# The first 256 tokens in two parts of 128: loads, norm and four small products

## The chip, the cores and the metric

The kernel runs on one core of a Trainium2 chip. The metric is the device time of one execution in microseconds (us). Engines: PE (TensorE, matrix products; PEld are its weight loads), DVE (VectorE), ACT (ScalarE), POOL (GpSimd) and SP (SyncE, which here only issues DMAs). SP and ACT each have a DMA queue of their own.

## The reference

`x` is 4 x 1024 tokens of 1024 features, float32. What matters of it:

```
xn = (x - mean) / sqrt(var + 1e-5)              # per token
g  = sigmoid(xn @ gate_w.T + gate_b)            # gate; then a linear recurrence over time gives s
h  = silu(silu(xn @ w1.T) @ w3.T) @ w2.T        # a small MLP, all 4096 tokens
p  = top-2 of softmax(xn @ wr.T), normed        # eight experts
out[expert] += p * h                            # adds to ROWS 0..7 of the output, by the expert's number
result = x + s * silu(out)                      # so only rows 0..7 differ from x
```

So nearly all work is in three products: `u` = xn by w1 and `m` by w3 over all tokens, and `g` by gate_w over the first 1024 tokens.

## The kernel before

**Tiles.** The tokens are taken in four groups of 1024. In each, a 1024 x 1024 x 1024 product is done as seven half-size products of sums and differences of quarters (i = 1 to 7, in the order 1, 2, 5, 6, 7, 4, 3), and most of these once more in seven. i = 1 of `u` is "plain": its eight small products are done as they are. A **small product** (`small`, L895) takes 256 tokens, 256 features and 256 output columns: four calls of `pe.matmul`, each with a stationary 128 x 128 of the weights and 256 moving token columns. Each call is two records in the profile, so a small product is 8 records. A `Half` (L911) holds one half-size product with its PSUM tiles `X`, `Z` and `Y`; its `step(n)` emits one small product and the DVE or ACT operation that takes the sum out of PSUM.

**The transposed input.** `xT` is stored with features along partitions. The block `first` (L1226), `[128, 4, 512]`, holds the first 512 tokens of the first 512 features: index 0 and 1 are token group 1 (tokens 0 to 255), 2 and 3 token group 2 (256 to 511). Each index has two tiles of 128 features ("k tiles") of 256 tokens. The features' mean and scale are per token, thus along the free axis here. To get them there, the statistics are taken from rows of `x` (tokens along partitions), a diagonal matrix is made of each (identity times the per-partition value), and a product of an all-ones matrix with the diagonal spreads the value over all partitions as a row in PSUM ("spread"). Then DVE subtracts the mean row and multiplies by the scale row (`on` in `first_tokens`, L359; `norm0`, L304).

**Order.** Every engine keeps the program's order (`Pinned`, L79). The order is written by hand: each step of a `Half` has a place (a number; `steps`, L1442), and `at(place, f)` puts anything else in a list that is emptied up to a place before the step of that place is emitted (`run_todo`, L191). A generator's `yield d` puts off its rest by `d` places. One place is about one small product.

**The start.** SP and ACT load `x_first` (rows 0 to 255 of `x`) in four pieces of 256 KB, two on each queue (L150). PE runs `warm(14)`, idle products on the identity (28 records), so that it is busy meanwhile (L1225). SP then loads, in this order (L1233 to L1240): index 0 of `first` (256 KB), half of the w1 block (the two indices 0 and 2, 512 KB), index 1 of `first`, the same half of the gate block, rows 256 to 511 of `x` in two pieces, the other halves of w1 and gate, indices 2 and 3 of `first`. From the ninth transfer on, SP waits before an issue until the transfer eight places before has landed (a wait on the same semaphore in the trace).

`first_tokens` (L317, place -10) then takes the statistics of all 256 tokens on DVE (four `bn_stats`, two `bn_aggr`), spreads mean and scale with `warm` products between, and norms index 0 and 1 in five DVE operations of 256 or 512 columns. `stats0` (L247) does the same for token group 2 at place -8, with its diagonals on ACT, and emits its two spreads 11.9 and 12.9 places later, so at places 3.9 and 4.9; `norm0` at 3.95 and 4.95 applies them, one DVE operation of 1024 columns each.

PE's small products in order: at places 0 and 1 `X_u` (two, accumulated), at 2 `X_g` and at 3 `Y_g`, all with token group 1 and the first halves of the weights; at 4 and 5 the two `Z_u`, with the second half of w1; at 6 and 7 the `X_u` of token group 2. ACT copies `X_u` and `X_g` out of PSUM after places 1 and 2; DVE adds `Y_g` at place 5.2. POOL's sums for later products (`first_sums`, `left_sums`) need the normed token group 2.

Of the kernel before, what the change touches and what calls it, by code (L numbers as in the profile page):

```python
# [10 lines left out]
F32 = mybir.dt.float32  # L11
# [5 lines left out]
P = 128  # L17
# [5 lines left out]
def kernel(  # L23
# [99 lines left out]
                self.home.append(self.tile)  # L123

    NB, NQ = 20, 18
    IDLE = 14
    blocks = deque(
        const.tile([P, 4, 2 * Q], F32, tag=f"b{i}", name=f"b{i}") for i in range(NB)
    )
# [18 lines left out]
    pool.memset(three_halves, 1.5)  # L148

    x_first = block()  # L150
    for n in range(2):
        for t, queue in ((0, sync), (1, act)):
            queue.dma_start(
                x_first[:, 2 * t + n, :], x[t * P : (t + 1) * P, n * H : (n + 1) * H]
            )

    root = const.tile([P, 1], F32, tag="root", name="root")
    act.activation(root, eps, AF.Sqrt)
# [83 lines left out]
    def part(t, a):  # L242
        return t[:, 2 * a : 2 * a + 2, :].rearrange("p b (k n) -> p (b k) n", n=Q)
# [3 lines left out]
    def stats0(I, a, xb, lag, wait=(0, 0), apart=0):  # L247

        mv = sp.tile([P, 2, 2], F32, tag="mv", name=f"mv_{I}{a}")
        for tt in range(2):  # L250
            xt = xb[:, 2 * tt : 2 * tt + 2, :]
            bn = sp.tile([P, 2, nc.vector.BN_STATS_DIM], F32, tag=f"bn{tt}", name=f"bn_{I}{a}{tt}")
            for n in range(2):
                dve.bn_stats(bn[:, n, :], xt[:, n, :])
            dve.bn_aggr(mv[:, tt, :], bn)
        xb.drop()
        dg = quarter()

        def diagonals(s, w):
            for tt in range(2):  # L260
                act.activation(
                    dg[:, (2 * s + tt) * P : (2 * s + tt + 1) * P],
                    ident,
                    AF.Identity,
                    scale=w[:, tt : tt + 1],
                )

        if (I, a) == (1, 1):
            bc = ps_sm.tile([P, 2, Q], F32, tag="sm", name="bc_11")
        elif (I, a) == (1, 0):  # L270
            bc = ps_y.tile([P, 2, Q], F32, tag="Y", name="bc_10")
        else:
            bc = acc.rearrange("p (s n) -> p s n", s=2)
        yield wait[0]

        sd, v, r1 = (bc[:, 1, 2 * i : 2 * i + 2] for i in range(3))
        act.activation(sd, mv[:, :, 1], AF.Sqrt, bias=eps)
        act.activation(v, mv[:, :, 1], AF.Identity, bias=eps)
        diagonals(0, mv[:, :, 0])
        r0 = sp.tile([P, 2], F32, tag="r2", name="r0")  # L280
        rs = sp.tile([P, 2], F32, tag="rs", name=f"rs_{I}{a}")
        dve.reciprocal(r0, sd)
        dve.reciprocal(r1, sd)
        dve.scalar_tensor_tensor(rs, r0, -0.5, r1, ALU.mult, ALU.mult)
        dve.tensor_mul(rs, rs, v)
        dve.scalar_tensor_tensor(rs, rs, 1.5, r1, ALU.add, ALU.mult)
        yield wait[1]
        diagonals(1, rs)
        yield lag
        for s in range(2):  # L290
            if s:
# [12 lines left out]
    def norm0(I, a, J, apart=0):  # L304
        p = part(xn[0, I, J], a)
        for s, op in ((0, ALU.subtract), (1, ALU.mult)):
            if s and apart:
                yield apart
            row = bc0[I, a][s].unsqueeze(1).to_broadcast([P, 4, Q])
            dve.tensor_tensor(p, p, row, op)  # L310

    def warm(n):

        for _ in range(n):
            pe.matmul(idle, ones, ident, start=True, stop=True, skip_group_check=True)

    def first_tokens():  # L317


        mv = sp.tile([P, 2, 2], F32, tag="mv", name="mv_00")  # L320
        bn = [
            sp.tile([P, 2, nc.vector.BN_STATS_DIM], F32, tag=f"bn{t}", name=f"bn_00{t}")
            for t in range(2)
        ]
        for n in range(2):
            for t in range(2):
                dve.bn_stats(bn[t][:, n, :], x_first[:, 2 * t + n, :])
        for t in range(2):
            dve.bn_aggr(mv[:, t, :], bn[t])
        x_first.drop()  # L330
        sd = sp.tile([P, 2], F32, tag="sd2", name="sd_00")
        act.activation(sd, mv[:, :, 1], AF.Sqrt, bias=eps)
        dg = quarter()
        rows = [
            ps_acc.tile([P, Q], F32, tag="rows", name="mean_00"),
            ps_sm.tile([P, Q], F32, tag="sm", name="scale_00"),
        ]
        bc0[0, 0] = rows

        def spread(s, w):  # L340
            d = dg[:, s * Q : (s + 1) * Q]
            for t in range(2):
                dve.tensor_scalar(
                    d[:, t * P : (t + 1) * P], ident, w[:, t : t + 1], None, ALU.mult
                )
            pe.matmul(rows[s], ones, d, start=True, stop=True, skip_group_check=True)

        spread(0, mv[:, :, 0])
        warm(2)
        v = sp.tile([P, 2], F32, tag="v2", name="v_00")  # L350
        dve.tensor_scalar(v, mv[:, :, 1], EPS, None, ALU.add)
        rs = sp.tile([P, 2], F32, tag="rs", name="rs_00")
        scales(rs, v, sd, 2)
        spread(1, rs)
        dg.drop()
        warm(3)
        p = part(xn[0, 0, 0], 0)

        def on(lo, hi, s, op):  # L359
            row = rows[s].unsqueeze(1).to_broadcast([P, hi - lo, Q])  # L360
            dve.tensor_tensor(p[:, lo:hi, :], p[:, lo:hi, :], row, op)

        on(0, 2, 0, ALU.subtract)
        on(0, 1, 1, ALU.mult)
        on(1, 2, 1, ALU.mult)
        on(2, 4, 0, ALU.subtract)
        on(2, 4, 1, ALU.mult)

    def stats(sb, bcs):

# [219 lines left out]
    def first_sums(t):  # L590

        for _ in fresh_sums("g", 1, t, False):
            yield 0.5
        yield 3
        for _ in left_sums("u", 0, 1, 1):
            yield 0.5

# [313 lines left out]
    class Half:  # L911
# [33 lines left out]
        def step(self, n):  # L945
# [9 lines left out]
            if self.plain:  # L955

                q = ((0, 1, 2, 3) if self.i == 1 else (0, 3, 1, 2))[n // 2]
                ps = self.X if n // 2 % 2 == 0 else self.Z
                go(ps, A[:, q // 2 * 2 + n % 2], t[:, n % 2 * 2 + q % 2], n % 2 == 0, n % 2 == 1)
                if n % 2:  # L960
                    self.first(q, ps)
            elif n == 0:
                go(self.X, A[:, 0], t[:, 0], True, False)
                self.first(0, self.X)
            elif n == 1:
                go(self.Z, s[0].tile, ts[0].tile, True, False)
                self.first(3, self.Z)
                s[0].drop()
                ts[0].drop()
            elif n == 2:  # L970
                go(self.X, s[1].tile, ts[1].tile, False, False)
                self.first(1, self.X)
                s[1].drop()
                ts[1].drop()
            elif n == 3:
                Y = ps_y.tile([P, 2 * Q], F32, tag="Y", name=f"Y_{self.tag}")
                go(Y, A[:, 1], t[:, 2], True, True)
                if (self.kind, self.i) == ("g", 1):
                    at(Y_AT, self.more, 0, Y)
                else:  # L980
                    self.more(0, Y)
            elif n == 4:
                go(self.X, s[2].tile, ts[2].tile, False, False)
                self.more(3, self.X)
                s[2].drop()
                ts[2].drop()
            elif n == 5:
                go(self.Z, s[3].tile, t[:, 3], False, True)
                self.more(1, self.Z)
                s[3].drop()  # L990
            elif n == 6:
                go(self.X, A[:, 3], ts[3].tile, False, True)
                self.first(2, self.X)
                self.whole(2)
                ts[3].drop()
# [237 lines left out]
    sync.dma_start(first[:, 0, :], xT[0, 0, 0, :, 0, :])  # L1233
    first_half("w1", 0)
    sync.dma_start(first[:, 1, :], xT[0, 0, 0, :, 1, :])
    first_half("gw", 0)
    load_x0(0, 1)
    first_half("w1", 1)
# [7 lines left out]
    at(-16, load_xn, 0, 1, 0, USES[1, 0] + G[1, 0])  # L1246
    at(-15, load_xn, 0, 1, 1, USES[1, 1] + G[1, 1])
    at(-10, first_tokens)
    at(-8, lambda: stats0(0, 1, x0[0, 1], 11.9, apart=1))
    at(3.95, norm0, 0, 1, 0, 1)  # L1250
    at(6, lambda: stats0(1, 0, x0[1, 0], 2.5, (1.5, 1)))
    at(6.5, norm0, 0, 0, 1)
    at(8.5, norm0, 0, 1, 1)
# [4 lines left out]
    at(18, norm0, 1, 1, 1)  # L1258
    at(26, consts)
    for IJ in HB:  # L1260
        at(0, lambda IJ=IJ: left.__setitem__(("u", 0, IJ), xn[(0,) + IJ]))

    halves = []
    for kind, sb, i, plain in line:
# [117 lines left out]
    def the_rest():  # L1382
# [60 lines left out]
        (at_first[kind, sb, i][n] if (kind, sb, i) in at_first else start[kind, sb, i] + 2 * n, k, n)  # L1443
        for k, (kind, sb, i, plain) in enumerate(line)
        for n in range(8 if plain else 7)
    )
    for place, k, n in steps:
        here[0] = place
# [81 lines left out]
```

## Time and profile before

| what | before |
|---|---|
| median of 3 runs | 820.97 us (820.76 to 821.0) |
| the profiled execution: its time | 820.79 us |
| its span on the core | 819.0 us |
| first real product on PE starts | 10.32 us |
| last record of PE starts | 814.43 us |
| DMA in the first 40 us | 381 GB/s |

The span is what the trace covers; some 1.8 us of the execution lie outside. All times below are from the span's start. In a timeline a line gives the start, the length, the engine, the source line, the operation with what it writes and reads, and how many records stand in the line; in brackets is the engine's idle time before it and what ended it. The recorded lengths of PE's products overlap: what counts there is the distance from one start to the next. All engine calls go through one helper, so that nearly every line has L89, and groups are told apart by the names of the tiles.

### The profile page before, as it was taken

The page shows a single profiled execution, that of the slowest core. Times are in us where ns is not written, and L with a number is a line of the kernel's source. Part 1 is how long each engine was busy: PE and PEld are TensorE (multiplying, and loading weights), DVE is VectorE, ACT ScalarE, POOL GpSimd, SP SyncE. Part 2 cuts the span into 40 slices and gives each one's busy share as a digit, 9 for nine tenths or more (in the row PEclk, how much of TensorE's full clock was granted, in tenths as well). Part 3 has the DMA queues.
Part 4 walks back from the last instruction along what each step waited for, and adds up shares of the span by engine and source line. Part 5 has one row for each costly group of instructions (what it writes and reads, how often), then busy time and mean ns, then how long its engine had stood idle before and what let it go on. Part 6 is the DMA issues. An engine that isn't in the chain of part 4 may idle for free.

```text
span 819.0 us, 11323 instructions
## 1 busy us (share of the span) xinstructions
PE 811.4 (99%) x4087; PEld 698.2 (85%) x4087; DVE 510.6 (62%) x872; ACT 267.3 (33%) x470; POOL 496.5 (61%) x398
## 2 busy tenths in 40 slices
PE   8999999999999999999999999999999999999997
PEld 7888888888888878888888788888888788888885
DVE  6986598765588534764985235666983246667643
ACT  2345126877233237341022065421122021220111
POOL 2799796957999394644547453754448454465300
PEclk9999999999999999999999999999999999999999
DMA  9946609464978958629955866559766355555700
GB/s 341 423 169 232 231 27 359 180 244 152 409 275 311 339 183 295 246 88 380 387 170 221 334 224 238 193 206 385 282 244 241 120 213 207 197 177 178 302 14 2
DMA packets 55927, 192.88 MB, mean 235 GB/s; under 512 B 6480, under 2 KB 9792, under 8 KB 44224
## 3 DMA queue, kind: packets, MB, share of 16 engines
q1 hardware_dynamic: 55552, 191.61, 63.6%
q8 instruction: 33, 0.54, 0.2%
q10 hardware_dynamic: 320, 0.54, 0.2%
q14 instruction: 22, 0.18, 0.1%
HBM read 169.01 MB, written 39.87 MB: 255 GB/s over the span
## 4 chain that ended last, share of the span: by engine, by line
PE 98%; DMA 1%; DVE 0%; issue 0%; SPq 0%; ACT 0%
PE X_u L89 24%; PE X_m L89 24%; PE Z_u L89 12%; PE Z_m L89 12%; PE Y_m L89 6%; PE X_g L89 6%; PE Y_u L89 6%; PE Z_g L89 3%; PE acc L89 2%; PE plT L89 2%; PE Y_g L89 1%; DMA b<-in_x 1%; PE pp L89 0%; PE bc L89 0%; DVE bn L89 0%; PE accB L89 0%
## 5 line engine op out<-in xcount | busy, mean ns | idle before, releaser
L89 POOL TENSOR_TENSOR q<-b 128x512 f32<-128x512 f32 x154 | 203.5, 1336 | 194.6 <-PE X_m L89 48.0
L89 ACT ACTIVATE b<-b 128x512 f32<-128x512 f32 (+1 forms) x152 | 105.4, 696 | 296.5 <-DVE b L89 292.5
L89 POOL TENSOR_TENSOR q<-b,q 128x512 f32<-128x512 f32 x98 | 133.7, 1368 | 7.2 <-issue 4.0
L89 POOL TENSOR_TENSOR b<-b,b 128x512 f32<-128x512 f32 x72 | 93.1, 1318 | 48.5 <-PE X_u L89 33.8
L89 DVE TENSOR_TENSOR b<-b,b 128x512 f32<-128x512 f32 x120 | 109.2, 924 | 2.7
L89 PE MATMUL X_m<-q,q 128*128 128x256 f32 x448 | 105.9, 379 | 0.0
L89 PE MATMUL X_u<-q,q 128*128 128x256 f32 x432 | 102.4, 380 | 0.0
L89 DVE TENSOR_TENSOR b<-X_u,b 128x512 f32<-128x512 f32 x87 | 60.1, 691 | 58.6 <-PE X_u L89 57.9
L89 DVE TENSOR_TENSOR b<-X_m,b 128x512 f32<-128x512 f32 x88 | 60.3, 687 | 56.9 <-PE X_m L89 56.6
L89 PEld LDWEIGHTS X_m<-q,q 128*128 128x128 f32 x448 | 85.0, 190 | 12.4 <-issue 0.8
L89 POOL TENSOR_TENSOR q<-q,b 128x512 f32<-128x512 f32 x56 | 73.7, 1317 | 32.3 <-PE X_u L89 25.1
L89 PEld LDWEIGHTS X_u<-q,q 128*128 128x128 f32 x432 | 81.8, 190 | 12.2 <-issue 1.2
L89 DVE TENSOR_TENSOR b<-b,bc 128x1024 f32<-128x1024 f32 x56 | 67.8, 1210 | 0.1
L89 PE MATMUL X_u<-b,b 128*128 128x256 f32 x248 | 58.4, 379 | 0.0
L89 PE MATMUL Y_m<-b,b 128*128 128x256 f32 x224 | 53.1, 380 | 0.0
L89 PE MATMUL Z_m<-b,q 128*128 128x256 f32 x224 | 53.0, 379 | 0.0
L89 PE MATMUL X_m<-b,b 128*128 128x256 f32 x224 | 52.9, 379 | 0.0
L89 PE MATMUL Z_m<-q,q 128*128 128x256 f32 x224 | 52.9, 379 | 0.0
L89 PE MATMUL X_m<-q,b 128*128 128x256 f32 x224 | 52.9, 379 | 0.0
L89 PEld LDWEIGHTS X_u<-b,b 128*128 128x128 f32 x248 | 47.0, 190 | 6.4
L89 DVE TENSOR_TENSOR b<-Z_u,b 128x512 f32<-128x512 f32 x47 | 32.5, 691 | 31.6 <-PE Z_u L89 30.9
L89 PE MATMUL Z_u<-q,q 128*128 128x256 f32 x216 | 51.1, 379 | 0.0
(182 smaller groups left out, 1179.2 us busy)
## 6 DMA issues: line engine op xcount, KB each, us to landing
q<-w SPq DMA_DIRECT2D x168, 256.0 KB, 4.5
b<-in_w SPq DMA_DIRECT2D x36, 1024.0 KB, 8.8
b<-w_T SPq DMA_DIRECT2D x24, 1024.0 KB, 6.2
b<-in_xT SPq DMA_DIRECT2D x15, 1024.0 KB, 11.6
w<-q SPq DMA_DIRECT2D x56, 256.0 KB, 7.1
b<-in_x SPq DMA_DIRECT2D x12, 1024.0 KB, 10.9
w_T<-b SPq DMA_DIRECT2D x8, 1024.0 KB, 4.4
b<-in_gw SPq DMA_DIRECT2D x6, 1024.0 KB, 15.6
```

Of the source, the lines that this page charges most:

```text
L89: r = f(*args, **kwargs)
```

## The change

`x_first` is loaded in another order: rows 0 to 127 come first, one piece on SP and one on ACT; the two pieces of rows 128 to 255 come later on SP, behind the first half of w1 and index 1 of `first`, and ahead of the gate half. `first_tokens` does everything for tokens 0 to 127, then for 128 to 255: statistics, diagonals, spreads and norm. The four small products of places 0 to 3 move into it, each in two halves of 128 token columns: all four first halves, then the second spreads, then all four second halves. Mean diagonals and the variance (plus eps) move from DVE to ACT. The idle products at the start go from 14 to 12. Token group 2's spreads come one place later (4.9 and 5.9), its norm at 4.96 and 5.96, and its multiply is split into two operations of 512 columns. Copies of `X_u` and `X_g` come at place 3.9. The left sums wait 0.6 places longer. The core of the diff:

```diff
-    IDLE = 14
+    IDLE = 12
...
-    for n in range(2):
-        for t, queue in ((0, sync), (1, act)):
-            queue.dma_start(
-                x_first[:, 2 * t + n, :], x[t * P : (t + 1) * P, n * H : (n + 1) * H]
-            )
+    def first_piece(queue, t, n):
+        queue.dma_start(x_first[:, 2 * t + n, :], x[t * P : (t + 1) * P, n * H : (n + 1) * H])
+    first_piece(sync, 0, 0)
+    first_piece(act, 0, 1)
...
@@ norm0 @@
-            row = bc0[I, a][s].unsqueeze(1).to_broadcast([P, 4, Q])
-            dve.tensor_tensor(p, p, row, op)
+            n = 2 if s and apart else 4
+            row = bc0[I, a][s].unsqueeze(1).to_broadcast([P, n, Q])
+            for k in range(0, 4, n):
+                dve.tensor_tensor(p[:, k : k + n], p[:, k : k + n], row, op)
...
@@ first_tokens @@
+        def moments(t):
+            for n in range(2):
+                dve.bn_stats(bn[t][:, n, :], x_first[:, 2 * t + n, :])
+            dve.bn_aggr(mv[:, t, :], bn[t])
+            act.activation(sd[:, t : t + 1], mv[:, t, 1:2], AF.Sqrt, bias=eps)
+            act.activation(diagonal(0, t), ident, AF.Identity, scale=mv[:, t, 0:1])
+            act.activation(v[:, t : t + 1], mv[:, t, 1:2], AF.Identity, bias=eps)
+            o = slice(t, t + 1)
+            scales(rs[:, o], v[:, o], sd[:, o], 1)
+            dve.tensor_scalar(diagonal(1, t), ident, rs[:, o], None, ALU.mult)
+        def spread(s, t):
+            pe.matmul(rows[s][:, t * P : (t + 1) * P], ones, diagonal(s, t), start=True, stop=True, ...)
+        def on(lo, hi, t, s):
+            c = slice(t * P, (t + 1) * P)
+            row = rows[s][:, c].unsqueeze(1).to_broadcast([P, hi - lo, P])
+            dve.tensor_tensor(p[:, lo:hi, c], p[:, lo:hi, c], row, (ALU.subtract, ALU.mult)[s])
+        def half_small(ps, A, B, t, start, stop):
+            for mt in range(2):
+                for kt in range(2):
+                    n = kt * Q + t * P
+                    pe.matmul(
+                        ps[:, mt * Q + t * P : mt * Q + (t + 1) * P],
+                        B[:, kt * Q + mt * P : kt * Q + (mt + 1) * P],
+                        A[:, n : n + P], ...)
+        moments(0)
+        spread(0, 0)
+        warm(2)
+        spread(1, 0)
+        warm(2)
+        four = ((hu.X, 0, hu.t[:, 0], True, False), (hu.X, 1, hu.t[:, 2], False, True),
+                (hg.X, 0, hg.t[:, 0], True, False), (Y, 1, hg.t[:, 2], True, True))
+        on(0, 2, 0, 0)
+        on(0, 1, 0, 1)
+        on(1, 2, 0, 1)
+        on(2, 4, 0, 0)
+        on(2, 4, 0, 1)
+        for n, (ps, q, B, start, stop) in enumerate(four):
+            half_small(ps, hu.A[:, q], B, 0, start, stop)
+            if n == 0:
+                moments(1)
+        spread(0, 1)
+        spread(1, 1)
+        for k in range(4):
+            for s in range(2):
+                on(k, k + 1, 1, s)
+        for ps, q, B, start, stop in four:
+            half_small(ps, hu.A[:, q], B, 1, start, stop)
+        at(3.9, hu.first, 0, hu.X)
+        at(3.9, hg.first, 0, hg.X)
+        at(Y_AT, hg.more, 0, Y)
...
@@ first_sums @@
-        yield 3
+        yield 3.6
...
@@ the loads on SP @@
     first_half("w1", 0)
     sync.dma_start(first[:, 1, :], xT[0, 0, 0, :, 1, :])
+    first_piece(sync, 1, 0)
+    first_piece(sync, 1, 1)
     first_half("gw", 0)
...
-    at(-8, lambda: stats0(0, 1, x0[0, 1], 11.9, apart=1))
-    at(3.95, norm0, 0, 1, 0, 1)
+    at(-8, lambda: stats0(0, 1, x0[0, 1], 12.9, apart=1))
+    at(4.96, norm0, 0, 1, 0, 1)
...
+        if not (k == 0 and n in (0, 1) or k == 1 and n in (0, 3))
```

More of the change, by code (lines that the diff above doesn't have):

```diff
@@ L257, in stats0, with diagonals @@
         dg = quarter()
-        def diagonals(s, w):
+        def diagonals(s, w, urgent=False):
             for tt in range(2):
[L261 to L266, printed above, removed]
+                d = dg[:, (2 * s + tt) * P : (2 * s + tt + 1) * P]
+                if urgent:
+                    dve.tensor_scalar(d, ident, w[:, tt : tt + 1], None, ALU.mult)
+                else:
+                    act.activation(d, ident, AF.Identity, scale=w[:, tt : tt + 1])
         if (I, a) == (1, 1):
@@ L278, in stats0 @@
         act.activation(v, mv[:, :, 1], AF.Identity, bias=eps)
-        diagonals(0, mv[:, :, 0])
+        diagonals(0, mv[:, :, 0], False)
         r0 = sp.tile([P, 2], F32, tag="r2", name="r0")
@@ L317, in first_tokens @@
     def first_tokens():
-        mv = sp.tile([P, 2, 2], F32, tag="mv", name="mv_00")
         bn = [
@@ L324, in first_tokens @@
         ]
[L325 to L330, printed above, removed]
+        mv = sp.tile([P, 2, 2], F32, tag="mv", name="mv_00")
         sd = sp.tile([P, 2], F32, tag="sd2", name="sd_00")
-        act.activation(sd, mv[:, :, 1], AF.Sqrt, bias=eps)
+        v = sp.tile([P, 2], F32, tag="v2", name="v_00")
+        rs = sp.tile([P, 2], F32, tag="rs", name="rs_00")
         dg = quarter()
@@ L338, in first_tokens @@
         bc0[0, 0] = rows
[L340 to L348, printed above, removed]
-        warm(2)
-        v = sp.tile([P, 2], F32, tag="v2", name="v_00")
-        dve.tensor_scalar(v, mv[:, :, 1], EPS, None, ALU.add)
@@ L352, in first_tokens @@
-        rs = sp.tile([P, 2], F32, tag="rs", name="rs_00")
-        scales(rs, v, sd, 2)
-        spread(1, rs)
-        dg.drop()
[L356 to L367, printed above, removed]
+        p = part(xn[0, 0, 0], 0)
@@ new lines, in first_tokens, with diagonal @@
+        hu, hg = halves[0], halves[1]
+        def diagonal(s, t):
+            n = s * Q + t * P
+            return dg[:, n : n + P]
+        def moments(t):
[8 more added lines that the diff above has]
+            dve.tensor_scalar(diagonal(1, t), ident, rs[:, o], None, ALU.mult)
@@ new lines, in spread @@
+        def spread(s, t):
+            pe.matmul(
+                rows[s][:, t * P : (t + 1) * P],
+                ones,
+                diagonal(s, t),
+                start=True,
+                stop=True,
+                skip_group_check=True,
+            )
+        def on(lo, hi, t, s):
+            c = slice(t * P, (t + 1) * P)
+            row = rows[s][:, c].unsqueeze(1).to_broadcast([P, hi - lo, P])
+            op = (ALU.subtract, ALU.mult)[s]
+            dve.tensor_tensor(p[:, lo:hi, c], p[:, lo:hi, c], row, op)
@@ new lines, in half_small @@
+        def half_small(ps, A, B, t, start, stop):
+            for mt in range(2):
+                for kt in range(2):
+                    n = kt * Q + t * P
+                    pe.matmul(
+                        ps[:, mt * Q + t * P : mt * Q + (t + 1) * P],
+                        B[:, kt * Q + mt * P : kt * Q + (mt + 1) * P],
+                        A[:, n : n + P],
+                        start=(start and t == 0 and mt == 0 and kt == 0),
+                        stop=(stop and t == 1 and mt == 1 and kt == 1),
+                        skip_group_check=True,
+                    )
@@ new lines, in first_tokens @@
+        hu.begin()
+        hg.begin()
+        moments(0)
+        spread(0, 0)
+        warm(2)
+        spread(1, 0)
+        warm(2)
+        Y = ps_y.tile([P, 2 * Q], F32, tag="Y", name="Y_g0_1")
+        four = (
+            (hu.X, 0, hu.t[:, 0], True, False),
+            (hu.X, 1, hu.t[:, 2], False, True),
+            (hg.X, 0, hg.t[:, 0], True, False),
+            (Y, 1, hg.t[:, 2], True, True),
+        )
+        on(0, 2, 0, 0)
+        on(0, 1, 0, 1)
+        on(1, 2, 0, 1)
+        on(2, 4, 0, 0)
@@ new lines, in first_tokens @@
+        on(2, 4, 0, 1)
[3 more added lines that the diff above has]
+                moments(1)
+        x_first.drop()
+        spread(0, 1)
+        spread(1, 1)
+        dg.drop()
+        for k in range(4):
[4 more added lines that the diff above has]
+        at(3.9, hu.first, 0, hu.X)
@@ L977, in step @@
                 go(Y, A[:, 1], t[:, 2], True, True)
[L978 to L981, printed above, removed]
+                self.more(0, Y)
             elif n == 4:
@@ L1260 @@
     for IJ in HB:
-        at(0, lambda IJ=IJ: left.__setitem__(("u", 0, IJ), xn[(0,) + IJ]))
+        at(-11, lambda IJ=IJ: left.__setitem__(("u", 0, IJ), xn[(0,) + IJ]))
     halves = []
```

## The prediction

> **What bounds the kernel now.** I read the page's shares first, then the busy times by stretches, then the chain of waits up to 12 us, then the engines' timelines around the first products.
>
> ```profile
> PE 811.4 (99%) x4087; PEld 698.2 (85%) x4087; DVE 510.6 (62%) x872; ACT 267.3 (33%) x470; POOL 496.5 (61%) x398
> ```
> ```profile
> 0.00:10.30 10.30, 7.16 (x42) 6.66 (x42) 5.82 (x20) 1.78 (x3) 1.32 (x12) 1.00 0.81 276
> 10.30:17.30 7.00, 7.00 (x34) 6.18 (x33) 5.15 (x14) 1.99 (x7) 1.22 (x1) 1.00 1.03 404
> ...
> 40.00:814.40 774.40, 774.13 (x3905) 665.41 (x3907) 478.98 (x803) 255.55 (x440) 475.84 (x371) 1.00 0.63 229
> ```
>
> The stretches give length, then busy time of PE, weight loads, DVE, ACT, POOL. From 10.30 us on PE is busy without a gap worth naming to 814.4. So the time is: when the first real product starts, plus PE's work, plus any hole that the change tears into it; nothing later can absorb a delay. The chain shows what sets the start:
>
> ```profile
> 1.20 4.66 DMA b<-in_x
> 5.86 0.02 issue
> 5.88 1.29 DVE bn L89 x2
> 7.17 0.24 DVE mv L89 x2
> ...
> 9.11 0.70 PE scale L89 x2
> 9.80 0.67 PE idle L89 x6
> 10.47 1.62 PE X_u L89 x7
> ```
>
> The statistics of 256 tokens wait for four transfers (5.86), then DVE works down to the scale row, and X_u starts. PE's timeline around it:
>
> ```profile
> 10.32 3.72 PE L89 MATMUL X_u<-b,b 128*128 128x256 f32 x16
> 13.88 1.89 PE L89 MATMUL X_g<-b,b 128*128 128x256 f32 x8
> 15.60 1.89 PE L89 MATMUL Y_g<-b,b 128*128 128x256 f32 x8
> 17.33 0.59 PE L89 MATMUL acc<-q,ones 128*128 128x256 f32 x2
> 17.76 1.89 PE L89 MATMUL Z_u<-b,b 128*128 128x256 f32 x8
> 19.49 0.59 PE L89 MATMUL acc<-q,ones 128*128 128x256 f32 x2
> 19.92 1.89 PE L89 MATMUL Z_u<-b,b 128*128 128x256 f32 x8
> 21.64 0.59 PE L89 MATMUL X_u<-b,b 128*128 128x256 f32 x2
> ```
>
> One small product is 8 records; start to start it takes 1.73 us (15.60 to 17.33), a record 0.216. The two "acc" spreads (token group 2's mean and scale) stand a whole product apart from each other, and the scale's spread stands a whole product ahead of X_u at 21.64, which needs it. That cover matters below. DVE there:
>
> ```profile
> 9.84 0.75 DVE L89 TENSOR_TENSOR b<-b,scale 128x256 f32<-128x256 f32 x2 [0.20 <-PE scale L89]
> ...
> 20.12 1.22 DVE L89 TENSOR_TENSOR b<-b,acc 128x1024 f32<-128x1024 f32 x1 [0.94 <-PE acc L89]
> 21.26 0.68 DVE L89 TENSOR_TENSOR b<-Y_g,b 128x512 f32<-128x512 f32 x1
> ```
>
> **Prices, from single records.** DVE tensor_tensor: 0.42 (256 columns), 0.68 (512), 1.22 (1024), near a straight line, so 128 columns 0.29 (estimate from these); a dependent one starts 0.035 after the other's end, an independent one 0.21 after its start. A DVE step on [128x2] with dependence: 0.20. Statistics: 0.61 per 512 columns, 0.71 from the last to the aggregate, 0.245 from that to ACT. ACT: 0.30 on [128x2], 0.20 to the next; 0.29 per diagonal, 0.39 long. DVE's end to PE's first record 0.05; PE's last record, 0.275 long with 128 columns and 0.38 with 256, to DVE 0.04; PE loses 0.10 when it restarts (10.317 to 10.637 against 0.216). The 128-column idle records follow each other by 0.111.
>
> **1. The earlier start.** The two first pieces stood at the heads of the two queues before (x rows 0-127 on SP, 128-255 on ACT) and landed at 4.52 and 4.70; now both belong to the first 128 tokens and I take the same times. DVE: 4.55 + 0.61 + 0.71 = 5.87 aggregate; ACT 6.11 root, 6.31 diagonal, 6.60 variance to 6.87 (now behind the diagonal); DVE product with it 6.90, 7.10, diagonal 7.30 to 7.59; PE spreads at 7.63, done 8.12; DVE 8.16 to 8.45; X_u at **8.50 instead of 10.32: -1.82**. The first half of w1 landed at 8.71 as the last of 1.75 MB; now it is the last of 1.25 MB, and that much had landed at 6.71. So it is there before 8.45; each tenth past that would come on top. Four idle records fewer end at 5.99; the gap to the mean at 6.74 is shorter than the 1.4 us of before, after which nothing ran slower.
>
> **2. More PE work.** Eight half products of 8 records at 0.111 are 7.14 for 6.91: +0.23; the four spread records of the second part now stand inside: +0.45. Together **+0.67**. Bounds for a 128-column record: 0.108 (half of 0.216) to 0.216; the idle record has the same shape, so I take it.
>
> The Trainium skill, "TensorE: Matmul & The Clock Gate", section "Back-to-back issue gap", speaks against halving columns: it gives about 81 ns a matmul at 128 columns in a stream of load-and-multiply pairs, and 262 cycles of 2.4 GHz at 256. By that a half would cost 0.74 of a whole and the change +3.3 us more (an estimate from the page). The idle row, 0.111 against 0.216, says 0.51 and decides.
>
> **3. The gate weights.** X_g used its weights at 13.7; now its first half is due at 8.60 + 2 x 0.89 = 10.38. With the x pieces moved up, the gate half is still the last of 2.5 MB, and landed at 10.75 (the third SP issue after 8.7 waits for it, at 10.77). So PE waits 0.39 and restarts: **+0.49**. Below: the DMA row sags between 7.0 and 8.5 us (219 to 314 GB/s against 400), 0.7 us lost; without that, 10.05 and no wait. Above: open. I take the row with the same bytes.
>
> **4. The second part's wait.** The four first halves end at S = 12.65. The second spreads come after them in PE's order; behind them PE has only the second halves, and those wait for DVE: mean at S+0.42, first multiply S+0.74 to S+1.03, PE S+1.09. The eight dependent 128-column steps (0.325 and 0.21 in turn) give the second k tile at S+1.57 and the fourth at S+2.63; PE, with three restarts, finishes the four halves at S+5.23, against S+0.45+3.57 without a wait: **+1.22**. With operations of 0.16 (the [128x2] row) it would be 0.54; with operations of 0.42 (the 256-column row), 2.27. Queued behind the waiting DVE are token group 2's statistics; they start at S+2.5 = 15.2, not 12.05, which counts in 5.
>
> **5. Token group 2 one place later.** Lag 11.9 to 12.9 puts the mean's spread ahead of the second Z_u and the scale's spread directly ahead of X_u. Statistics to mean diagonal take 4.2 us (12.05 to about 16.2), so S+6.7 against PE's need at S+6.96: covered by 0.28. But after the scale's spread PE has nothing: 0.63 to DVE, 0.68 for the first half of the multiply (split in two, which is why not 1.22), 0.05, restart 0.10 is 1.46 where the spread alone took 0.43: **+1.03**. If that multiply could run in 0.42 it would be 0.77; unsplit 1.57.
>
> **What costs nothing.** Diagonals go to ACT, idle until 15.0. The Y_g sum moves in front of the multiply: DVE is free from S+8.8 to S+9.7 for its 0.68. Left sums on POOL start about 2.3 us later, need 5.1, and POOL sat idle 26.5 to 30.6. The later norms have 1.4 us before their spread (diagonals 28.85, spread 30.28). The remaining SP issues wait for landings that do not come later.
>
> **Sum.** -1.82 + 0.67 + 0.49 + 1.22 + 1.03 = +1.59. Check: X_u's third product starts at S+10.55 = 23.2 instead of 21.65. The profiled execution took 820.79 (span 819.0 and 1.8 around it), giving 822.4; the median of the runs shown is 0.18 above it, so 820.97 + 1.59 = **822.5**, +0.19%.
>
> **Rivals.**
> *Gate weights in time.* They land by 10.3. For it: the sag may belong to the order of before. Then part 3 is 0, but the second scale diagonal (12.45) comes 0.1 late: +1.2, 822.2.
> *Slower: loads bind harder.* Every tenth that the gate half lands after 10.8 is a tenth on the end, and from 10.81 on the loss is over 0.2%. At 12.05, where the next half megabyte landed before: +2.9, 823.9. For it: a transfer of ACT's queue moves to SP's, which then carries nearly all; against: from 8.5 to 12 us SP alone moves 400 GB/s.
> *Not slower: early loads.* If the first pieces have the engines to themselves and everything lands earlier, S is bound only by the gate half plus 1.88; it must land by 9.2 to undo the loss. Price 820.9 or less. Against: two 256 KB heads landed at 4.5 before too.
> *The split norm is hidden after all.* If 128-column steps cost 0.16, part 4 falls to 0.54: 821.9.
>
> **How the numbers follow.** A measurement here can tell about 0.2%, 1.64 us, from no change: slower begins at 822.61. Forecast case 0.50 (822.1 to 822.9); weights in time 0.20 (821.8 to 822.4); loads bind harder 0.16 (822.7 to 823.9); hidden norm 0.09; early loads 0.05. Slower: 0.24 of the forecast case and 0.16, 0.40. Faster by over 0.2% would need the early loads and a hidden norm together: 0.02. Same: 0.58. The range leaves out the early loads and the far halves of the hidden norm and of the hard loads: 821.3 to 823.3.
>
> **What would show it.** X_u first at 8.4 to 8.6; a PE hole of 0.3 to 0.6 before X_g, released by the DMA of in_gw; holes before and within the second X_u halves released by DVE; the last spread before the whole X_u with about 0.9 idle behind it; everything after shifted by one amount. Wrong it is if PE stays dense at one of these places, if the X_u start is past 8.7 (a load), or if a hole opens after 25 us.

## The result and the profile after

The changed kernel takes 823.35 us (median of 7 runs, 823.09 to 824.0) against 820.76 (7 runs, 820.62 to 821.08) of the kernel before beside it: +2.59 us, ratio 1.0031 (95% interval 1.0022 to 1.0041). It is slower, and 0.05 us beyond the upper end of the predicted range; 822.5 was forecast. The profiled execution took 823.77 us (span 822.0), 0.42 above the median.

PE's timeline of the changed kernel, from the first product to the place where the prediction summed up (start, length, what it writes and reads, records, and in brackets the idle time before it with its releaser):

```profile
8.34 1.13 PE L89 MATMUL X_u<-b,b 128*128 128x128 f32 x8
10.05 1.16 PE L89 MATMUL X_u<-b,b 128*128 128x128 f32 x8 [0.57 <-DVE b L89]
11.90 1.16 PE L89 MATMUL X_g<-b,b 128*128 128x128 f32 x8 [0.70 <-DMA b<-in_gw]
12.90 1.06 PE L89 MATMUL Y_g<-b,b 128*128 128x128 f32 x8
13.79 0.39 PE L89 MATMUL mean<-q,ones 128*128 128x128 f32 x2
14.01 0.39 PE L89 MATMUL scale<-q,ones 128*128 128x128 f32 x2
14.95 2.49 PE L89 MATMUL X_u<-b,b 128*128 128x128 f32 x16 [0.55 <-DVE b L89]
17.28 1.06 PE L89 MATMUL X_g<-b,b 128*128 128x128 f32 x8
18.17 1.06 PE L89 MATMUL Y_g<-b,b 128*128 128x128 f32 x8
19.06 1.89 PE L89 MATMUL Z_u<-b,b 128*128 128x256 f32 x8
20.88 0.67 PE L89 MATMUL acc<-q,ones 128*128 128x256 f32 x2
21.38 1.89 PE L89 MATMUL Z_u<-b,b 128*128 128x256 f32 x8
23.11 0.59 PE L89 MATMUL acc<-q,ones 128*128 128x256 f32 x2
24.53 3.69 PE L89 MATMUL X_u<-b,b 128*128 128x256 f32 x16 [0.83 <-ACT b L89]
```

The first product starts 1.98 us sooner than before, and the third `X_u` product 2.89 us later (24.53 against 21.64). In between stand four holes: before the second `X_u` half, before `X_g`, before the second halves, and before the third `X_u`. The bracket shows less than the hole costs, since the last record's modelled end reaches into it; start to start, less the record's own distance, they are 0.74, 0.86, 0.71 and 0.99, each with a restart of 0.08 to 0.10. The stretches show that nothing more is lost or won behind (length, then busy time of PE, weight loads, DVE, ACT, POOL; clock, DMA share, GB/s):

```profile
8.34:24.53 16.19, 13.51 (x88) 11.60 (x89) 11.32 (x33) 4.16 (x12) 5.00 (x4) 1.00 1.04 411
24.53:40.00 15.47, 15.47 (x72) 13.63 (x73) 14.23 (x30) 5.71 (x16) 11.54 (x10) 1.00 1.01 419
40.00:817.40 777.40, 777.13 (x3922) 668.02 (x3921) 481.68 (x806) 256.24 (x441) 478.37 (x373) 1.00 0.63 229
```

PE's last record starts at 817.40 instead of 814.43, 2.97 later: what is lost by 24.53 us is the result. The chain of waits that the prediction showed began with the load of x and the statistics. Now it is this:

```profile
3.97 7.89 DMA b<-in_gw
11.86 0.04 issue
11.90 1.16 PE X_g L89 x8
13.06 0.89 PE Y_g L89 x8
```

The statistics are no longer on it. What sets the end is the landing of the gate weights at 11.86.

### The profile page after: what moved, and what is told of

It is laid out like the page before. It is cut to its first block, busy times and chain, and to the rows that moved or that the text cites. A ratio compares the mean times of both kernels' runs of the same rounds, so it can differ in the third digit from the quotient of the medians.

```text
span 822.0 us, 11401 instructions
## 1 busy us (share of the span) xinstructions
PE 813.1 (99%) x4117; PEld 699.3 (85%) x4117; DVE 511.8 (62%) x882; ACT 268.7 (33%) x475; POOL 496.2 (60%) x398
## 4 chain that ended last, share of the span: by engine, by line
PE 98%; DMA 1%; SPq 0%; DVE 0%; issue 0%; ACT 0%; DVEq 0%
PE X_m L89 24%; PE X_u L89 24%; PE Z_u L89 12%; PE Z_m L89 12%; PE X_g L89 6%; PE Y_m L89 6%; PE Y_u L89 6%; PE Z_g L89 3%; PE acc L89 2%; PE plT L89 2%; PE Y_g L89 1%; DMA b<-in_gw 1%; PE pp L89 0%; SPq L89 0%; PE bc L89 0%; DVE b L89 0%
## 5 line engine op out<-in xcount | busy, mean ns | idle before, releaser
L89 PE MATMUL X_u<-b,b 128*128 128x256 f32 (+1 forms) x264 | 59.5, 368 | 2.1 <-DVE b L89 1.1
## 6 DMA issues: line engine op xcount, KB each, us to landing
b<-in_xT SPq DMA_DIRECT2D x15, 1024.0 KB, 11.6
```

The costliest lines, as they stand in the source:

```text
L89: r = f(*args, **kwargs)
```

## The experiments

Theory at the start: the five terms are right but for the third, since the gate half landed 1.11 us later than the 10.75 that I had taken from the kernel before. Rivals: the changed order delays w1 or the gate by its own bytes, and another order wins; or the other terms, above all the two on DVE, are mis-sized and cancel. Gains below are differences of the distance to the kernel before, which ran beside each (medians 820.76 to 820.95). The intervals of E2, E9, E11, E12 and E14 overlap those of the kernels that they are set against, so a gain is read from the medians together with the holes in the profiled executions.

### E1: only token group 2 late, in the kernel before

```diff
-    at(-8, lambda: stats0(0, 1, x0[0, 1], 11.9, apart=1))
-    at(3.95, norm0, 0, 1, 0, 1)
+    at(-8, lambda: stats0(0, 1, x0[0, 1], 12.9, apart=1))
+    at(4.96, norm0, 0, 1, 0, 1)
# besides: norm0's multiply in two, left sums 3.6, both as in the change; the rest as before
```

> The kernel before with only the last part of the change: token group 2's spreads and norm one place later, its multiply split in two, the left sums 0.6 places later. Theory (part 5 of the prediction): PE stays dense from 10.32 to the second group-2 spread and then has nothing until DVE has multiplied half a block, a hole of about 0.93 us and a restart of 0.10 before X_u, so +1.0 us against the kernel before (821.8), and nothing else moves. Rival (the hole only shows because group 2's statistics are late in the changed kernel): here the statistics are early, so no hole, +0.0.

821.79 against 820.78, +1.01; ratio 1.0010 (1.0001 to 1.0020). The one new hole:

```profile
21.07 0.59 PE L89 MATMUL acc<-q,ones 128*128 128x256 f32 x2
22.49 1.75 PE L89 MATMUL X_u<-b,b 128*128 128x256 f32 x7 [0.83 <-ACT b L89]
```

1.42 from spread to product where the spread alone takes 0.43. The fifth term, predicted at 1.03, is shown, alone and in full.

### E2: second spreads ahead of `Y_g`'s first half, in the changed kernel

```diff
         for n, (ps, q, B, start, stop) in enumerate(four):
+            if n == 3:
+                spread(0, 1)
+                spread(1, 1)
             half_small(ps, hu.A[:, q], B, 0, start, stop)
```

> The changed kernel with the spreads of tokens 128 to 255 moved ahead of the last first half (Y_g) in PE's order, nothing else. Theory (part 4): the wait of 1.22 us between first and second halves is there only because nothing stands behind the spreads; with 0.89 us of Y_g behind them it falls to about 0.4, so 0.8 us faster than the changed kernel (about 822.5), with Z_u after it that much earlier. Rival (the second halves are held by something else, the loads or DVE's statistics): the holes stay, 0.0 to 0.2 us faster.

822.68, ratio 1.0026 (1.0016 to 1.0035): 0.69 nearer to the kernel before. The half product covers DVE's first two steps, and the hole of 0.71 before the second halves is gone; inside them 0.03 and 0.05 are left, with restarts of 0.10. The wait of the fourth term is real, and most of it came from the place of two spreads.

### E3, E5, E8: other orders of the first loads, in the changed kernel

```diff
# E3: the four x pieces first, two on each queue, as before; the rest on SP
# E5: the gate half on ACT's queue, behind ACT's x piece
# E8: x rows 128 to 255 on ACT's queue, behind ACT's x piece
```

> The changed kernel with the loads in the order of before: all four pieces of x first, two on each queue, now with both pieces of tokens 0 to 127 at the heads. Theory (the order of the loads is what the prediction mis-sized): w1's half lands at 8.7, index 1 at 9.4, the gate half at 10.75 as in the kernel before; X_u starts at 8.8 instead of 8.34, the hole before the second X_u half is 0.6 instead of 0.74, the one before X_g is gone, so the first halves end at about 13.15 instead of 13.79: 0.6 us faster than the changed kernel (about 822.7). Rival (the engines are slow in this stretch whatever the order): the gate half still lands near 11.9 and the time is that of the changed kernel.

> The changed kernel with the first half of the gate weights on ACT's queue, behind its one piece of x, instead of eighth on SP. Theory (one queue alone is slow from about 4 to 8.5 us; with two busy queues the same stretch moves 350 to 400 GB/s, as the kernel before showed up to 6 us): all transfers of the head land by about 9.5, the gate half at 7 to 8.5, so the hole of 0.86 us before X_g is gone and the one before the second X_u half is smaller: 1.0 us faster than the changed kernel, 822.3. Rival (the engines are slow until 8.5 us whatever the queues): the gate half is early only at w1's expense; X_u starts at 9 or later, the sum lands no earlier than 10.5 and the time is within 0.4 us of the changed kernel.

> The changed kernel with the two pieces of x for tokens 128 to 255 on ACT's queue instead of SP's, a probe of the loads. Theory (SP alone is slow): ACT's queue is busy until about 6, the engines move 350 to 400 GB/s until then, w1's half lands near 8.2 still (it shares the engines), but index 1 and the gate half land 0.5 to 1.0 us earlier than in the changed kernel (9.1 and 11.9). Rival (slow until 8.5 whatever the queues): the gate half lands within 0.4 us of 11.9.

| run | w1 half | xT index 1 | gate half | `X_u` starts | time, ratio |
|---|---|---|---|---|---|
| changed kernel | 8.21 | 9.09 | 11.86 | 8.34 | 823.35, 1.0031 |
| E3 | 9.12 | 9.79 | 11.13 | 9.26 | 823.52, 1.0042 (1.0029 to 1.0056) |
| E5 | 9.18 | 9.79 | 8.91 | 9.31 | 823.61, 1.0041 (1.0027 to 1.0055) |
| E8 | 8.94 | 9.64 | 10.97 | 9.08 | 823.36 (one run) |

(Landings in us; the trace has 16 landing marks for a transfer, and the last one counts.) In all three the hole before `X_g` is gone, and no time is gained: w1 lands 0.7 to 1.0 later, and PE waits for it in front of `X_u` instead. My gains of 0.6 for E3 and 1.0 for E5 were wrong; E5 went as its rival said, and in E8 w1 came at 8.94 instead of near 8.2. In these three runs a transfer on ACT's queue only changed which product waits.

### E4: w1's and gate's halves exchanged

```diff
-    first_half("w1", 0)      # third load of SP
+    first_half("gw", 0)
...
-    first_half("gw", 0)      # seventh
+    first_half("w1", 0)
```

> The changed kernel with the first halves of w1 and gate exchanged in SP's order (gate third, w1 eighth), a probe of the loads alone: X_u now waits for w1. Theory A (the slow stretch belongs to the bytes of w1): gate, third in line, passes at 400 GB/s and lands near 6.7, and the slow stretch comes with w1 at the end. Theory B (it belongs to the place or the time, between 3.5 and 8.5 us, once SP's queue is alone): gate lands near 8.2 as w1 does in the changed kernel, and w1 near 11.9. The time is longer than the changed kernel's by 2 to 3 us either way.

The gate half in w1's place landed at 7.48, w1 in the gate's at 11.41 (826.78, one run; `X_u` must wait for w1). That is between theory A (6.7) and theory B (8.2) for the gate, and w1 in the last place was late in its turn. So the lateness is not bound to one array's bytes; one run says no more.

### E6 and E7: the scale spread of group 2 in the middle of the second `Z_u`

```diff
+        bc0[I, a][1] = halves[1].Z[:, 0:Q]      # the scale row, in Z_g's bank
...
+            if mt and amid:
+                amid.pop()()                      # the spread, amid a small product
# E7: the same with E5's loads; both hold E2's edit
```

> The kernel with the early spreads (second spreads ahead of Y_g's first half) and besides: group 2's scale spread stands in the middle of the second Z_u, in a PSUM bank of its own (the one Z_g uses later), and the Y_g sum comes behind the multiply on DVE. Theory (part 5: nothing covers the multiply because the spread stands directly ahead of its user): half a product, 0.86 us, now covers it, the hole of 0.99 us before the third X_u falls to about 0.15: 0.85 us faster than with the early spreads alone, 821.8. Rival: DVE's mean subtraction (1.22 us) then ends last and the hole stays at 0.6 or more: 822.4.

> Gate half on ACT's queue, early spreads and the split second Z_u together. Theory (the three holes are separate terms of one sum on PE): 1.0 + 0.7 + 0.85 us faster than the changed kernel, 820.8, level with the kernel before or up to 0.5 us faster. Rival (an earlier PE meets the next wait, token group 2's diagonals, whose rows of x land at 13 to 14 us): part of it is given back ahead of the spread of group 2, 821.5.

828.68 (ratio 1.0095, 1.0079 to 1.0110) and 828.15 (1.0091, 1.0076 to 1.0107): far off what was expected. The hole before the third `X_u` did fall to 0.16, but E6's PE shows a new one:

```profile
26.35 1.89 PE L89 MATMUL Z_u<-b,b 128*128 128x256 f32 x8
32.76 3.51 PE L89 MATMUL Z_g<-q,q 128*128 128x256 f32 x8 [4.51 <-DVE b L89]
36.06 2.07 PE L89 MATMUL X_g<-q,q 128*128 128x256 f32 x8
```

DVE reads the scale row once more for the next norm of token group 2 (31.39 to 32.61), and until then `Z_g` can't write its own bank. I had thought only of the row's first reader. The product that waited then took 3.30 us, start to start, for 1.73.

### E9 and E10: the row in a free half bank, then x rows on ACT's queue

```diff
-            bc0[I, a][1] = halves[1].Z[:, 0:Q]
+            bc0[I, a][1] = row_bank[0][:, Q:H]    # other half of the first mean row's bank
# E10: the same with E8's loads
```

> The kernel of the second spreads moved ahead of Y_g's first half (822.68), and token group 2's scale spread in the middle of the second Z_u product, as in the split-Z run, but with its row in the unused half of the bank that holds the first group's mean, so that Z_g's bank is free. Theory (what slowed the split-Z run is the bank alone; the hole before the third X_u product is the spread's place): the hole falls from 0.99 to about 0.16, as it did there, Z_g waits for nothing, and the time is 822.68 - 0.8 = 821.9, about 1.1 over the kernel before. Rival (the first group's norms read the same bank, so the spread or the norm waits, or the sum of Y_g that now stands behind the multiply holds a later product): another hole of 0.5 or more between 20 and 35 us, and 822.4 or more.

> The run before, with the x rows 128 to 255 on ACT's queue. Theory (the 2.5 MB of the head land at about 11 us in every order, and an order only chooses which product waits): X_u starts at about 9.0 with about 1.0 of holes behind it, no hole before X_g, and the time is within 0.4 of the run before: 821.5 to 822.3. Rival (the SP queue alone is what costs; two queues give 0.7): 821.2 or less, at or near the time of the kernel before.

E9: 821.92, ratio 1.0011 (1.0002 to 1.0021), 0.93 nearer than E2, with no wait at `Z_g` and 0.16 before the third `X_u`. The bank was the whole trouble of E6. E10: 822.31, 1.0015 (1.0006 to 1.0024), 0.01 above the band expected and against its rival: the gate half landed at 10.50, no hole stands before `X_g`, but w1 came at 8.46 and xT index 1 at 9.16. DVE norms index 1 before it takes the second statistics, so the second scale diagonal ends at 13.0, and its spread waits for it:

```profile
12.17 0.49 PE L89 MATMUL mean<-q,ones 128*128 128x128 f32 x2
13.06 0.49 PE L89 MATMUL scale<-q,ones 128*128 128x128 f32 x2 [0.40 <-DVE q L89]
```

### E11: the changed kernel without the wait for the gate half

```diff
-            (hg.X, 0, hg.t[:, 0], True, False), (Y, 1, hg.t[:, 2], True, True),
+            (hg.X, 0, hu.t[:, 0], True, False), (Y, 1, hu.t[:, 2], True, True),
```

> The changed kernel, with X_g and Y_g multiplied by the half of w1 that is there, in place of the gate weights' half: it leaves out the first gate product's first quarter pair, and all instructions stay. Theory (the hole of 0.86 and its restart of 0.10 before X_g are a full loss, because nothing behind it has slack): the second spreads start about 0.9 earlier (the second scale diagonal was ready at 13.0, the spread would stand at 13.05), and the time is 0.9 less than the changed kernel's, 822.4. Rival (the second part's statistics or loads would hold the second spreads anyway): the hole moves to the second spreads, and less than 0.4 is gained.

822.86, ratio 1.0021 (1.0012 to 1.0030): 0.68 nearer, 0.9 was expected. In its profiled execution the hole before `X_g` is gone and the four first halves end at 13.07 instead of 13.79; xT index 1 came late in it (9.34), and the hole before the second `X_u` half is 0.87 instead of 0.74. So the wait for the gate half is shown to cost time, up to the next wait, which is again a load.

### E12, E13, E14: w1's half on ACT's queue

```diff
     first_piece(sync, 0, 0)
     first_piece(act, 0, 1)
+    act.dma_start(first_w1[:, 0::2, :], w1[0, 0][:, 0::2, :])   # and no longer third on SP
# E12: in E9.  E14: in the changed kernel, alone.
# E13: in E9, and x rows 128 to 255 behind it on ACT's queue
```

> The row-bank run with w1's first half on ACT's queue behind the x piece, so that SP's queue carries 1.75 MB and ACT's 0.75 MB. Theory (an order only moves the wait): w1 and xT land within 0.5 of 8.7 and 9.2, the gate half at 10.6 to 11.2; X_u starts at 8.4 to 9.1 and the waits between 8 and 12 us sum to 0.8 to 1.5; the time is 821.3 to 822.1. Rival (one queue alone is the cause of the late landing): waits of 0.3 or less in sum, X_u at 8.3, and 820.8 or less.

> The run with w1's half on ACT's queue, and x rows 128 to 255 behind it on ACT's queue too: 1.25 MB on each queue up to the gate half. Theory A (SP's queue alone is what makes the head's 2.5 MB late, and an even split undoes it): the gate half lands at 10.6 or before, no hole before X_g, and the waits of 0.4 before X_g go: 821.0. Theory B (a queue's start is slow in any split, and an order only moves the wait): x rows 128 to 255 stand behind w1 and land at 10 or later, so the second statistics and spreads come later by what X_g gains: 821.3 to 822.0.

> The changed kernel with one edit: w1's half on ACT's queue. Theory A (the late landing is the price of one queue alone, and is the term of the sum that was mis-sized): the hole before X_g falls from 0.86 to 0.3 to 0.4, the one before the second X_u half from 0.74 to 0.2 or less, X_u starts 0.3 to 0.6 later, and the time is 0.5 below the changed kernel's: 822.8, near the predicted 822.5. Rival (order only moves the wait): the time is the changed kernel's, 823.3 to 823.6, with the wait in front of X_u.

E14: 823.04, ratio 1.0022 (1.0013 to 1.0031), 0.50 nearer than the changed kernel, as theory A had it by this distance; the median itself is 0.2 above its 822.8. In its profiled execution `X_u` starts 0.55 later, no hole stands before the second `X_u` half, and 0.46 is left before `X_g` (0.3 to 0.4 was expected). E12 against E9, 11 runs each on the same chip: 821.39 (820.99 to 821.62) against 821.92 (821.52 to 822.58), 0.53. E12's time lies in the band of its theory that an order only moves the wait (821.3 to 822.1), and its landings fit that theory; its rival, one queue alone as the cause, asked for 820.8 or less. E12 can't be told from the kernel before (ratio 1.0000, 0.9991 to 1.0009; its median is 0.44 above 820.95). Its PE:

```profile
8.92 2.02 PE L89 MATMUL X_u<-b,b 128*128 128x128 f32 x16 [0.36 <-DVE b L89]
11.09 1.16 PE L89 MATMUL X_g<-b,b 128*128 128x128 f32 x8
12.08 0.39 PE L89 MATMUL mean<-q,ones 128*128 128x128 f32 x2
...
22.05 2.18 PE L89 MATMUL X_u<-b,b 128*128 128x256 f32 x9
```

`X_u` starts later than in the changed kernel (8.92 for 8.34; the bracket names DVE, but w1 landed at 8.83, after DVE's step), yet it runs through, the hole before `X_g` is 0.31 (gate half at 11.05), and the third `X_u` is at 22.05. The even split, E13, is worse again: 823.68, 1.0032 (1.0020 to 1.0044). The gate half came at 10.99, but the last x piece behind w1 at 11.73, and the second spreads waited 1.34 and 0.57 for the statistics. That is theory B's wait, but the time is 1.7 above the upper end of its band (822.0), and theory A, an even split that undoes the late landing (821.0), failed. No version here beats the kernel before.

**What the runs say together.** By these distances the 2.59 us of the change part into 0.69 for the place of the second spreads (E2), 0.93 for token group 2's scale spread (E9), 0.53 for w1's half on ACT's queue (E12), and 0.44 that stay. These are steps taken one on top of the other. E12's step changes the place of w1 among the loads together with its queue, so it doesn't tell which of the two gained; and E12's interval holds 1.0000, so the last 0.44 can't be told from nothing.

## Why the prediction was wrong, and where it was right

**1, the earlier start: right.** -1.82 was predicted, -1.98 measured (8.34). The x pieces landed at 4.14 and 4.31, and w1's half, at 8.21, was "there before 8.45" as said, though 1.50 later than the 6.71 taken for its bytes; it, and not DVE (ready at 8.07), then set the start.

**2, more PE work: right.** From 8.34 to 13.79, less the holes and restarts (0.74 + 0.86 + 0.20 + 0.07), 32 records take 3.58: 0.112 each for 0.111. The Trainium skill, "TensorE: Matmul & The Clock Gate", section "Back-to-back issue gap", gives 81 ns at 128 columns as a sustained figure and 262 cycles at 256 as an isolated one; from the two the prediction made a half product 0.74 of a whole one (an estimate). The isolated figures of the section for both, 134 and 262 cycles, would make it 0.51. Here a half takes 0.89 against 1.73, that is 0.51.

**3, the gate weights: this step failed.** It read: "With the x pieces moved up, the gate half is still the last of 2.5 MB, and landed at 10.75", and "I take the row with the same bytes". The bytes are the same, the landing isn't: 11.86 in the profiled execution. From there the rest follows: 11.86 + 0.04, two half products of 0.89 and the restart make 13.79 for the end of the first halves, where 12.65 was predicted: 1.14 too late, of which the landing is 1.11. The rival that named it, *loads bind harder*, also priced it: a tenth for a tenth, 823.9 at 12.05, hence 823.7 at 11.86; the execution took 823.77. I gave it 0.16, and held against it that SP alone moves 400 GB/s from 8.5 us on. It does; but the loss lies earlier. That the wait costs time is shown by E11, which leaves it out and gains 0.68. Why the landing is late stays open; this is what the runs show of it. Here are the stretches of the kernel before, then of the changed one (last columns: clock, DMA share, GB/s):

```profile
4.00:6.00 2.00, 2.00 (x17) 2.00 (x17) 1.40 (x3) 0.00 (x0) 0.00 (x0) 1.00 1.01 358
8.50:12.00 3.50, 3.39 (x21) 2.90 (x20) 3.15 (x8) 0.00 (x0) 0.00 (x0) 1.00 1.05 420
```
```profile
4.00:6.00 2.00, 2.00 (x14) 2.00 (x14) 1.49 (x3) 0.28 (x2) 0.00 (x0) 1.00 0.80 198
8.50:12.00 3.50, 2.23 (x17) 1.85 (x16) 2.44 (x6) 0.50 (x3) 0.00 (x0) 1.00 1.04 413
```

From 4 to 6 us the rate is 198 GB/s instead of 358. By queue (packets, MB, share of the 16 engines), before and then changed, in this same stretch:

```profile
q1 hardware_dynamic: 247, 0.45, 65.8%
q10 hardware_dynamic: 149, 0.27, 34.9%
```
```profile
q1 hardware_dynamic: 212, 0.40, 79.7%
```

SP's queue (q1) carried nearly the same in both, 0.45 and 0.40 MB; ACT's (q10) came on top, 0.27 MB, and in the changed kernel it is empty by then. But this stretch can be slow with work on both queues too (E12, the first row; E8, E10, E13 and E14 moved 224 to 250 GB/s), and E4 moved 330 with SP's queue alone (the second row):

```profile
4.00:6.00 2.00, 2.00 (x14) 2.00 (x14) 1.44 (x3) 0.00 (x0) 0.00 (x0) 1.00 0.77 249
4.00:6.00 2.00, 2.00 (x12) 2.00 (x12) 1.50 (x3) 0.28 (x2) 0.00 (x0) 1.00 1.02 330
```

Over all profiled executions, between 4 and 8.5 us: with nothing but SP's queue 1.15 to 1.24 MB (five runs; E4 moved 1.34), with work on both 1.33 to 1.49 (ten runs). The 2.5 MB were complete at 11.41 to 12.14 with SP alone (six runs), and at 10.50 to 11.24 with both (nine; E13's 11.73 falls out). So a lone queue goes with a landing some 0.7 us later on the mean (11.7 against 11.0, E13 among them), with E4's 1.34 MB inside the other group. The edit that I counted as a mere change of order also takes one piece of 256 KB from ACT's queue to SP's; that this move made the landing late is likely, but not shown: E3 puts the pieces back, the gate half lands at 11.13, and no time is gained, and E12's gain came with another order. Packets took up to 0.87 us in the slow stretch against a usual 0.08, and nothing tells what they waited for. The lag is uneven: the first of the 16 landing marks of the gate half came at 9.97 (9.79 before), the last at 11.86 (10.75), so 0.93 of the 1.11 lies between the first mark and the last.

Part of the miss is the spread from one execution to the next. E1 has the load order of before, and its gate half landed at 11.24; so the 10.75 that I took was the earlier of two. Five executions in the changed order (the changed kernel, E2, E6, E9, E11) had it at 11.50 to 12.14. The third term should have been a range of landings, not one row.

The Trainium skill, "DMA: Bandwidth & Descriptors", section "Issuing engines are not separate DMA queues", says that issuing on several engines saves only the sequencer's issue time. From 8.5 us on the rows agree (SP alone, 413 GB/s). Before that the runs don't decide: the sums from 4 to 8.5 us speak against it, and E3, E5 and E8, which gained no time, for it.

In the medians the miss is smaller: +2.59 for the +1.59 of the forecast. Of the 1.00, 0.19 is the fifth term below, which leaves some 0.8 for the landing, hence about 11.6 (an estimate), inside the range of the five executions.

The prediction also did not expect xT index 1 to bind. It landed at 9.09, and PE waited 0.74 for the norm behind it. In the changed kernel that cost nothing of its own, since the gate half came later still; in E10 and E11 it was what stood next.

**4, the second part's wait: right.** The holes behind the second spreads are 0.71, 0.20 and 0.04 with restarts of 0.10, together 1.25; 1.22 was predicted. All four second halves take 5.27 from the mean's spread on; 5.23 was predicted. The rival of the hidden norm fell: DVE's eight steps follow each other at 0.31 and 0.21 in turn (0.39 the first time), 0.28 to 0.29 long.

```profile
15.12 0.29 DVE L89 TENSOR_TENSOR b<-b,scale 128x128 f32<-128x128 f32 x1
15.33 0.28 DVE L89 TENSOR_TENSOR b<-b,mean 128x128 f32<-128x128 f32 x1
15.64 0.29 DVE L89 TENSOR_TENSOR b<-b,scale 128x128 f32<-128x128 f32 x1
```

**5, token group 2 one place later: right, with a small slip.** 0.99 and a restart of 0.08, so 1.07 for 1.03, and E1 gave 1.01 by itself. The mean's spread, "covered by 0.28", was not: it waits 0.08 and restarts at another 0.08, so that the third `X_u` comes at 10.74 behind the first halves instead of 10.55.

**The sum.** Four of five terms held within 0.2 us. The third put the end of the first halves 1.1 too early in the profiled execution, and as nothing behind the head has slack, all of it arrived at the end.

## What to carry to other kernels

When a change moves transfers, don't take a landing from one execution and the bytes ahead of it: the gate half, the last of the same 2.5 MB, landed at 10.75 and 11.24 in the order of before and at 11.50 to 12.14 in five executions of the changed one. That fewer queues at work go with later landings is a reason for a wider range; as a cause it is not shown. Where a start is bound by loads, an earlier first product can just move the wait to the next operand, as here; list the landing of every operand against its first use before counting the gain. And a product cut in two needs work for PE between a spread and its reader: two spreads moved ahead of one half product, and one into the middle of another, gave back 1.6 of 2.6 us.

## What the runs showed that was not expected

A long wait of PE costs more than itself. E6 by stretches (PE busy is the first number after the length, the clock the third from the end):

```profile
28.00:32.00 4.00, 0.24 (x2) 0.00 (x0) 3.83 (x9) 0.91 (x3) 0.48 (x1) 1.00 1.01 422
33.00:36.00 3.00, 3.00 (x8) 2.35 (x8) 2.37 (x6) 0.00 (x0) 3.00 (x3) 0.50 1.00 418
36.00:37.00 1.00, 1.00 (x5) 0.82 (x4) 0.00 (x0) 0.58 (x1) 1.00 (x2) 0.79 1.04 434
```

After 4.5 us without work the granted clock is 0.50 for 3.4 us (33.0 to 36.4), and eight records take 3.30 instead of 1.73; so some 1.6 of E6's loss is clock and not wait. E4's PE, after 3.4 us of idling for w1, shows the same (0.50 from 12.7 to 16.1 us), and so does E7's after 4.1 us (32.3 to 35.7). The gaps of up to 1.4 us in the other runs left the clock at full.
